# A two-layer graph attention kernel: sixteen early gathers are kept in SBUF until layer 1 begins, and their completion is placed anew over the groups

## The chip, the core and the metric

The kernel runs on one core of a Trainium2 chip. The time is the device time of one execution in microseconds. Before the change the median of five runs was 2100.81 us, the lowest 2096.71 and the highest 2101.95. Engines are named as in the profile: PE multiplies matrices, DVE and ACT work on vectors, POOL issues the gathers, and SP issues the plain transfers. Each engine takes its instructions in order, so whatever waits at the head of a queue holds up everything behind it.

## The reference

There are 6250 nodes with 768 features and 100000 edges, sorted by destination. The features are normalised and rectified, then pass through two attention convolutions, two dense layers and a residual:

```python
def gat_conv(x, src, dst, W, a_src, a_dst, bias, heads):
    h = (x @ W).reshape(n, heads, -1)
    e = leaky_relu(alpha_s[src] + alpha_d[dst], 0.2)     # per edge and head
    e = exp(e - segment_max(e, dst)[dst])
    alpha = e / (segment_sum(e, dst)[dst] + 1e-16)
    return segment_sum(h[src] * alpha[:, :, None], dst).reshape(n, -1) + bias

h = relu(layernorm(x))
h = relu(gat_conv(h, ..., heads=4))     # 768 -> 4 * 64, called layer 1
h = relu(gat_conv(h, ..., heads=1))     # 256 -> 256, called layer 2
out = x + relu(h @ Wm1 + bm1) @ Wm2 + bm2
```

Each layer also adds one loop edge per node. The costly access is `h[src]`, one row of a node table for every edge.

## The kernel before

**Tiles.** Nodes are cut into NT = 49 tiles of 128. Edges are cut into tiles of 128, two tiles make a pair, and four tiles make a group; there are 196 groups. Four groups belong to a node tile, with t the node tile and j the place of a group in it (g = 4t + j).

**The feature stage** is the loop over i in 0 to 48 at lines 509 to 552. It computes the rows `h` of node tile i on PE (line 447), scales them into `kept[i]` on ACT, and stores them from SP to the node table in DRAM (`store1`, line 474). SP also loads `x` eight tiles ahead (line 202) and its transposed copy `xT` five tiles ahead (line 410). In the program as built, SP's transfers share eight completion semaphores in turn, so an issue waits until the transfer eight places before it has landed. POOL's gathers have eight of their own.

**Layers 1 and 2** are both `layer_edges`. For every tile of 128 edges POOL issues one indirect DMA (`gather`, line 645), which fetches the 128 source rows into half of a pair buffer `G`. Gathers are issued `AHEAD` = 8 groups before their use. DVE forms the edge weights of a pair from its rows (lines 712 to 724), PE sums the rows by destination (line 736), and the finished node tiles go through `Node1.steps` or `Node2.steps`. The buffers `G` are one ring of 20 (`gathered`, line 257), which the early gathers of the next paragraph share.

**Early gathers (SOON).** POOL has little to do in the feature stage, so 23 pairs of layer 1 are gathered there. Pair i belongs to group 8i + 11. It is gathered as soon as only the first `SOON[i]` node tiles are in the table (`soon_rows`, line 352); an edge whose source is later fetches a row that is dropped afterwards. The number of tiles still missing runs from 20 down to 2, so the pairs are gathered one or two per iteration from i = 28 to i = 46. To free its buffer the pair is copied to DRAM (`soon_away`, line 360, from SP), and read back eight groups before its use (`soon_back`, line 364). In layer 1 each half of such a pair, numbered k = 2i and 2i + 1, is completed: SP fetches the source numbers (`soon_sources`, line 371), DVE compares them with the node numbers of the missing tiles (`soon_hits`, line 379), PE multiplies the resulting hits with the `kept` tiles (`soon_missing`, line 389), and DVE adds the product to the gathered rows (`soon_whole`, line 396).

**When the copies go out before.** In the feature stage a pair is copied out in the iteration that is `SOON_HELD` = 6 tiles after its gather, so from i = 34 on, right after the store of tile i. Of the 23 pairs, 18 are copied there. The other five are copied by `soon_away(NT)` at line 804, when layer 1 begins, behind the loads of layer 1's first tables.

**The order in SP's queue** in iteration i is: `x` of tile i + 8, `xT` of tile i + 5, the store of tile i, and then the copies. At the beginning of layer 1 it is: two weight loads (lines 924 and 170), three loads `drow` of the destination numbers (line 610), the source numbers of the first pair, the copies, the fourth `drow`, and four copies of edge masks (line 664).

**When the completion runs before.** Half k is completed over node tile t = k: hits at j = 0, the product at j = 2, and the addition at j = 1 of the next tile.

Of the kernel before, what the change touches and what calls it, by code (L numbers as in the profile page):

```python
# [27 lines left out]
NT = -(-N // P)  # L28
# [22 lines left out]

SOON = [NT - m for m in (11, 20, 2, 19, 11, 18, 3, 17, 4, 16, 4, 15, 5, 15, 6, 14, 7, 13, 8, 12, 9, 18,
                         10)]
SOON_AT = {2 * (8 * i + 11) + 1: i for i in range(len(SOON))}
SOON_FROM, SOON_HELD = min(SOON), 6
BARE = 8


# [11 lines left out]
def kernel(  # L70
# [21 lines left out]
    nc = tc.nc  # L92
# [11 lines left out]
    def bcast(src, n, off=0):  # L104

        return bass.AP(tensor=src.tensor, offset=src.offset + off, ap=[[0, P], [1, n]])
# [103 lines left out]
    def heads_row(row):  # L210
        return row[:, :RW[1]].rearrange("p (h c) -> p h c", h=4)
# [124 lines left out]
    soon_d = dram.tile([len(SOON), P, 2 * TW[1]], F32, name="soon_d")  # L336
    soon_G, soon_of, soon_p, soon_hit = {}, {}, {}, {}
    soon_pair = {i: pair for pair, i in SOON_AT.items()}

# [13 lines left out]
                        out=soon_G[i][:, t], out_offset=None, in_=table[1][:there * P],  # L353
                        in_offset=bass.IndirectOffsetOnAxis(ap=soon_i[:, i, t:t + 1], axis=0))

    def soon_away(there):

        for i in sorted(soon_G):
            if SOON[i] <= there:
                nc.sync.dma_start(soon_d[i], soon_G.pop(i).rearrange("p t c -> p (t c)"))  # L360

    def soon_back(i):
        G = rows_in(1)
# [3 lines left out]
    def soon_sources(pool, i):  # L367

        if i < len(SOON):
            soon_of[i] = pool.tile([P, 2 * P], I32, name="soon_of", bufs=2)  # L370
            nc.sync.dma_start(soon_of[i], bcast(src_rows, 2 * P, 2 * P * soon_pair[i]))

    def soon_hits(pool, k):

        i, t = divmod(k, 2)
        if i < len(SOON):
            m = NT - SOON[i]
            soon_hit[k] = pool.tile([P, NT - SOON_FROM, P], F32, name="soon_hit")
            nc.vector.tensor_tensor(  # L379
                soon_hit[k][:, :m],  # L380
                soon_of[i][:, t * P:(t + 1) * P].unsqueeze(1).to_broadcast([P, m, P]),
                nid_ps[:, SOON[i]:].unsqueeze(2).to_broadcast([P, m, P]), ALU.is_equal)

    def soon_missing(k):
        if 0 <= k < 2 * len(SOON):
            there, hit = SOON[k // 2], soon_hit.pop(k)
            soon_p[k] = ps.tile([P, TW[1]], F32, name="missing1", tag="n")
            for T in range(there, NT):
                nc.tensor.matmul(soon_p[k], hit[:, T - there], kept[T], start=(T == there),  # L389
                                 stop=(T == NT - 1))  # L390

    def soon_whole(G, k):
        if 0 <= k < 2 * len(SOON):
            i, t = divmod(k, 2)
            row = G[soon_pair[i]][:, t]
            nc.vector.scalar_tensor_tensor(row, row, soon_ok[:, i, t:t + 1], soon_p.pop(k),
                                           ALU.mult, ALU.add)
# [3 lines left out]
    with tc.tile_pool(name="w1p", bufs=1) as wp, tc.tile_pool(name="x1", bufs=6) as xp, \  # L401
# [3 lines left out]
        def fetch_x(i):  # L405
            xs[i], _ = load_x(xp, i)
# [102 lines left out]
        for i in range(NT):  # L509
            h = features1(i)  # L510
            if i == 0:
                centre(1)
                moments(2)
            elif i == 1:
                centre(2)
                moments(3)
                spread_means(3)
                moments(4)
            else:
                if i + 3 < NT:  # L520
                    moments(i + 3)
                if i + 2 < NT:
                    spread_means(i + 2)
                if i + 1 < NT:
                    centre(i + 1)
            if i == 0:
                fetch_x(6)
                fetch_x(7)
            if i + 8 < NT:
                fetch_x(i + 8)  # L530
            if i + 5 < NT:
                fetch_xT(i + 5)
            if i == 40:
                first_places()
            if 2 <= i < 2 + KI // 2:
                for k in range(2 * i - 4, 2 * i - 2):
                    nc.vector.tensor_reduce(w1[:, k, HID:], score_w[k], AX.X, ALU.add)
            if BARE <= i < 2 * BARE:
                scores1(i - BARE)
            keep1(i, *h)  # L540
            if 4 <= i < BARE + 4:
                halves[i - 4] = halve(heads_row(kept[i - 4])[:, :, :HID // 4])
            if BARE < i <= 2 * BARE:
                store1(i - BARE - 1)
            if BARE < i <= SOON_FROM - 3:
                store1(i - 1)
            if i >= SOON_FROM - 3:
                store1(i)
                soon_rows(i + 1)
                soon_away(i + 1 - SOON_HELD)  # L550
            if i >= 10:
                next(pieces, None)

# [65 lines left out]
    def layer_edges(layer, H, node, pre, matched, pre_pool):  # L619
# [4 lines left out]
        with tc.tile_pool(name=f"eg{layer}", bufs=5) as eg, \  # L624
# [3 lines left out]
            G, hot, e_ps, o_ps = {}, {}, {}, {}  # L628
# [5 lines left out]
            def gather(g):  # L634
                if not 0 <= g < NG:
                    return
                for t in tiles(g):
                    k = TPG * g + t
                    soon = layer == 1 and k // 2 in SOON_AT
                    if k // 2 not in G:  # L640
                        G[k // 2] = (soon_back(SOON_AT[k // 2]) if soon else
                                     first_G.get(layer, {}).get(k // 2) or rows_in(layer))
# [10 lines left out]
            def make_mask(u):  # L653

                if not 0 <= u < NU:
                    return
                if layer == 2:
                    return fetch_mask(u + 1)
                a, b = (t * P for t in both(u))
                mask[u] = maskp.tile([P, 8 * P], BF16, name="mask")  # L660
                at = u % 2 * 8 * P
                nc.vector.tensor_scalar(mask[u][:, a:b], drow[u // 2][:, at + a:at + b], pidx, None,
                                        ALU.is_equal)
                nc.sync.dma_start(mask_d[u * P:(u + 1) * P, a:b], mask[u][:, a:b])
# [135 lines left out]
            if layer == 1:  # L800
                for r in range(3):
                    fetch_rows(r)
                soon_sources(pre_pool, 0)
                soon_away(NT)
                fetch_rows(3)
                for u in range(4):
                    make_mask(u)
# [37 lines left out]
            for g in range(NG):  # L845
                t, j = divmod(g, 4)
                if layer == 2 and g >= NG - 2:
                    if g == NG - 2:
                        last_pairs()
                    continue  # L850
                if g == NG - 2:
                    at_end.append(g)
                gather(g + AHEAD)
                pair(g, 0)
                if g == NG - 1:
                    pair(g, 1)
                if g == NG - 2:
                    gather_up(NU - 2)
                advance(g)
                if taken_up(2 * g) is not None:  # L860
                    gather_up(taken_up(2 * g))
                if g <= NG - 4:
                    make_hot(g + 1)
                if g in (NG - 4, NG - 3):
                    make_hot(g + 2)
                if j == 0:
                    if layer == 1:
                        fetch_rows(t + 4)
                        if t % 2:
                            soon_sources(pre_pool, (t + 1) // 2)  # L870
                    node.prefetch(t)
                    meet(t + 1)
                    if layer == 1:
                        soon_hits(pre_pool, t)
                elif j == (2 if t < NT - 1 else 1):
                    node.ahead(t)
                    if layer == 1:
                        soon_missing(t)
                elif j % 2:
                    if layer == 1 and j == 1:  # L880
                        soon_whole(G, t - 1)
                    make_mask((g + 7) // 2)
                if g == NG - 3:
                    idle_ps.append(ps.tile([P, 4 * P], F32, name="idle_ps", tag="e"))
                if g >= NG - 3:
                    stay_warm(3)
                if g < NG - 1:
                    pair(g, 1)
                advance(g, 1)
                if j == 3:  # L890
                    join(t + 1)
                if taken_up(2 * g + 1) is not None:
                    gather_up(taken_up(2 * g + 1))
                if NG - 3 <= g < NG - 1:
                    stay_warm(3)
                hot.pop(g, None)
                if layer == 1 and g == NG - 6:
                    first_sources(2)
# [534 lines left out]
```

## Time and profile before

| what | value |
|---|---|
| median of five runs | 2100.81 us |
| the profiled execution | 2099.1 us |
| its span | 2097.3 us |
| PE busy | 1665.6 us (79%) |
| POOL busy | 1523.4 us (73%), 1666 instructions |
| DVE busy | 1412.2 us (67%) |
| ACT busy | 408.6 us (19%) |
| granted PE clock, mean | 0.889 |
| first gather of the feature stage | 99.31 us |
| first gather of layer 1 | 168.82 us |
| first gather of layer 2 | 1094.62 us |
| start of the last gather | 2073.61 us |

Times inside the execution count from the start of the span. The profile calls an engine busy only while an instruction runs on it; the time between two DMA issues of POOL that wait for nothing is shown as idle with the releaser "issue". A line of a timeline gives the start, the duration, the engine, the line of the code, the operation, what is written and read, the number of instructions merged, and in brackets the idle time ahead of it with what ended it. SPq is SP's queue.

### The profile page before, as it was taken

What the parts mean: (1) busy time and instruction counts of PE and PEld (TensorE: products, weight loads), DVE (VectorE), ACT (ScalarE), POOL (GpSimd) and SP (SyncE); (2) the same over time, 40 slices, a digit from 0 to 9 for tenths busy, and PEclk for the clock granted to TensorE, in tenths of its full rate; (3) what the DMA queues carried; (4) which work ended last, traced back from release to release, by engine and by line L of the source; (5) the groups of instructions that cost most, each with busy time, mean ns of one, the idle gap of its engine ahead of it and who ended that gap; (6) DMA issues with size and microseconds to landing.
All of it is one profiled execution on the core that took longest, in us unless ns stands there. A gap on an engine that the chain in (4) does not pass through costs nothing. (4 is left out here: it accounts for less than half of the span.)

```text
span 2097.3 us, 26497 instructions
## 1 busy us (share of the span) xinstructions
PE 1665.6 (79%) x7727; PEld 1212.1 (58%) x7729; DVE 1412.2 (67%) x4195; ACT 408.6 (19%) x1273; POOL 1523.4 (73%) x1666
## 2 busy tenths in 40 slices
PE   9986878887887888878867777778778777777877
PEld 6864756666665666666645545545455455454544
DVE  7856888888887888888876655555555555555554
ACT  5761111111111111111111111111111111111211
POOL 7057777777777777777777777777777777777774
PEclk9997999989998998999989888888888888888899
DMA  9998666666666666666557455555555555555553
GB/s 347 347 374 282 175 193 177 185 187 179 190 178 187 185 181 182 181 186 185 162 142 223 131 182 177 161 182 165 175 182 156 182 172 166 182 160 179 169 178 108
DMA packets 167328, 400.37 MB, mean 191 GB/s; under 512 B 36631, under 2 KB 54254, under 8 KB 167174
## 3 DMA queue, kind: packets, MB, share of 16 engines
q0 software_dynamic: 75072, 211.10, 37.6%
q1 hardware_dynamic: 90732, 185.99, 24.8%
q10 hardware_dynamic: 1370, 1.48, 0.2%
q8 instruction: 65, 1.06, 0.2%
q14 instruction: 89, 0.73, 0.1%
HBM read 333.87 MB, written 64.56 MB: 190 GB/s over the span
## 5 line engine op out<-in xcount | busy, mean ns | idle before, releaser
L645 POOL DMA_INDIRECT G<-table,src_i x1507 | 1431.3, 950 | 459.6 <-issue 325.6
L736 PE MATMUL o_ps<-G,hw 128*128 128x258 f32 x1564 | 463.6, 434 | 234.7 <-DVE hw L719 233.6
L736 PE MATMUL o_ps<-hw,hot 128*128 128x260 f32 x1564 | 454.3, 433 | 159.1 <-DVE hw L724 135.1
L736 PEld LDWEIGHTS o_ps<-G,hw 128*128 128x128 f32 x1564 | 315.5, 214 | 353.0 <-DVE hw L719 285.8
L712 DVE TENSOR_TENSOR e_ps<-G,e_ps 128x8 f32<-128x8 f32 (+1 forms) x782 | 129.1, 165 | 527.5 <-DMA G<-table,src_i 522.9
L736 PEld LDWEIGHTS o_ps<-hw,hot 128*128 128x128 f32 x1564 | 306.3, 208 | 275.1 <-DVE hw L724 193.1
L762 ACT ACTIVATE sum<-acc 32x260 f32<-32x260 f32 (+1 forms) x384 | 159.9, 416 | 1396.0 <-DVE acc L753 1335.2
L719 DVE TENSOR_SCALAR hw<-iota_ps,dcol,w 128x128 f32<-128x128 f32 x782 | 284.9, 406 | 14.5
L724 DVE TENSOR_TENSOR hw<-G,e_ps 128x520 f32<-128x520 f32 x391 | 271.9, 696 | 13.4
L389 PE MATMUL missing<-kept,soon_hit 128*128 128x268 f32 x1028 | 250.7, 402 | 0.0
L389 PEld LDWEIGHTS missing<-kept,soon_hit 128*128 128x128 f32 x1028 | 201.2, 200 | 37.0
L1085 PE MATMUL y_ps<-wm,mT 128*128 128x384 f32 x392 | 199.2, 643 | 0.0
L447 PE MATMUL h_ps<-w,r 128*128 128x264 f32 (+1 forms) x588 | 137.4, 387 | 10.0 <-ACT r L437 9.9
L673 DVE TENSOR_TENSOR hot<-iota_ps,dcol 128x512 f32<-128x512 f32 x196 | 133.5, 681 | 0.0
L447 PEld LDWEIGHTS h_ps<-w,r 128*128 128x128 f32 x588 | 108.3, 191 | 32.2 <-ACT r L437 13.2
L1085 PEld LDWEIGHTS y_ps<-wm,mT 128*128 128x128 f32 x392 | 85.8, 242 | 62.8 <-issue 38.6
L352 POOL DMA_INDIRECT G<-table,soon_i x46 | 43.9, 954 | 78.3 <-DMA xt<-in_x 53.0
L753 DVE SCALAR_TENSOR_TENSOR acc<-acc,keep,o_ps 128x260 f32<-128x260 f32 (+1 forms) x192 | 91.2, 475 | 0.9 <-PE o_ps L736 0.9
L379 DVE TENSOR_TENSOR soon_hit<-soon_of,iota_ps 128x1408 f32<-128x1408 int32 (+18 forms) x46 | 75.2, 1635 | 9.5 <-PE missing L389 9.5
L722 DVE TENSOR_TENSOR e_ps<-e_ps,G 128x8 f32<-128x8 f32 x391 | 68.0, 174 | 13.6 <-DVE e_ps L712 0.2
L715 DVE TENSOR_TENSOR w<-e_ps,G 128x2 f32<-128x2 f32 x391 | 62.1, 159 | 14.3 <-DVE e_ps L712 1.1
L435 DVE TENSOR_TENSOR cent<-xTt,mean_ps 128x768 f32<-128x768 f32 x49 | 46.6, 951 | 32.2 <-PE mean_ps L429 17.6
(415 smaller groups left out, 1180.4 us busy)
## 6 DMA issues: line engine op xcount, KB each, us to landing
xt<-in_x SPq DMA_DIRECT2D x96, 384.0 KB
drow<-dmod_d SPq DMA_DIRECT2D x49, 512.0 KB
mask_d<-mask SPq DMA_DIRECT2D x97, 256.0 KB
mask<-mask_d SPq DMA_DIRECT2D x97, 256.0 KB
G<-table,src_i POOLq DMA_INDIRECT x1507
xTt<-in_xT SPq DMA_DIRECT2D x49, 384.0 KB
out<-y SPq DMA_DIRECT2D x48, 384.0 KB
table<-kept SPq DMA_DIRECT2D x49, 134.0 KB
```

Source lines behind the costliest of these rows:

```text
L379: nc.vector.tensor_tensor(soon_hit[k][:, :m], soon_of[i][:, t * P:(t + 1) * P].unsqueeze(1).to_broadcast([P, m, P]), nid_ps[:, SOON[i]:].u ...
L389: nc.tensor.matmul(soon_p[k], hit[:, T - there], kept[T], start=(T == there), stop=(T == NT - 1))
L447: nc.tensor.matmul(h_ps[:, :n], r[:, k], w1[:, k, :n], start=(k == 0), stop=(k == KI - 1))
L645: nc.gpsimd.indirect_dma_start(out=G[k // 2][:, k % 2], out_offset=None, in_=table[layer], in_offset=bass.IndirectOffsetOnAxis(ap=src_i[:, ...
L673: nc.vector.tensor_tensor(hot[g][:, T[0]:T[0] + n], iota_ps.unsqueeze(1).to_broadcast([P, n, P]), dcol[:, k:k + n].unsqueeze(2).to_broadca ...
L712: nc.vector.tensor_mul(v, e2, rho)
L719: nc.vector.tensor_scalar(hw[:, t], iota_ps, dcol[:, k:k + 1], w[:, t], ALU.is_equal, ALU.mult)
L724: nc.vector.tensor_mul(hw, Gp[:, :, :RW[1]].rearrange("p t (h c) -> p t h c", h=H), w.unsqueeze(3).to_broadcast([P, 2, H, C + 1]))
L736: nc.tensor.matmul(o_ps[u], l, r[:, :RW[layer]], start=(g % 2 == 0 and k == 0), stop=(g % 2 == 1 and k == tiles(g)[-1]))
L753: nc.vector.scalar_tensor_tensor(acc, run[0], keep[:, u % 2:u % 2 + 1], o_ps.pop(u), ALU.mult, ALU.add)
L762: nc.scalar.activation(done[t][r], acc[r], AF.Copy)
L1085: nc.tensor.matmul(y_ps, mT[:, j], wm2[:, j, s * half:(s + 1) * half], start=False, stop=(j == KH - 1))
```

## The change

Three things change.

1. `soon_away` now takes the number of pairs that may stay. It copies out the oldest ones until no more than that are left. `SOON_HELD` becomes 16, so in the feature stage the first copy goes out in iteration 41, when the 17th pair is gathered; seven pairs are copied by iteration 46. The other 16 are copied when layer 1 begins, oldest first.
2. The steps that complete a half are tied to the group `at` = 8i + 11 of the pair rather than to the node tile. The source numbers are fetched at `at` - 13. The first half has its hits at `at` - 10, its product at `at` - 8 and its addition at `at` - 6; before these were at `at` - 11, - 9 and - 6. The second half has them at `at` - 6, - 5 and - 3; before at `at` - 7, - 5 and - 2. Hits therefore fall on groups with j = 1, where an edge mask is made too, and no longer on those with j = 0.
3. `dynamic_dma_scratch_size`, the bytes per SBUF partition reserved for the descriptors of POOL's DMAs, is 4096 and no longer 8192.

```diff
-SOON_AT = {2 * (8 * i + 11) + 1: i for i in range(len(SOON))}
-SOON_FROM, SOON_HELD = min(SOON), 6
+SOON_GROUP = [8 * i + 11 for i in range(len(SOON))]
+SOON_AT = {2 * g + 1: i for i, g in enumerate(SOON_GROUP)}
+SOON_FROM, SOON_HELD = min(SOON), 16
...
-    def soon_away(there):
-
-        for i in sorted(soon_G):
-            if SOON[i] <= there:
-                nc.sync.dma_start(soon_d[i], soon_G.pop(i).rearrange("p t c -> p (t c)"))
+    def soon_away(held):
+
+        for i in list(soon_G)[:max(len(soon_G) - held, 0)]:
+            nc.sync.dma_start(soon_d[i], soon_G.pop(i).rearrange("p t c -> p (t c)"))
...
-                soon_away(i + 1 - SOON_HELD)
+                soon_away(SOON_HELD)
...
-                soon_away(NT)
+                soon_away(0)
...
                     if layer == 1:
                         fetch_rows(t + 4)
-                        if t % 2:
-                            soon_sources(pre_pool, (t + 1) // 2)
                     node.prefetch(t)
                     meet(t + 1)
-                    if layer == 1:
-                        soon_hits(pre_pool, t)
                 elif j == (2 if t < NT - 1 else 1):
                     node.ahead(t)
-                    if layer == 1:
-                        soon_missing(t)
                 elif j % 2:
-                    if layer == 1 and j == 1:
-                        soon_whole(G, t - 1)
                     make_mask((g + 7) // 2)
+                if layer == 1:
+                    for i, at in enumerate(SOON_GROUP):
+                        for k, hits_at in ((2 * i, at - 10), (2 * i + 1, at - 6)):
+                            if g == hits_at + 3 + (k % 2 == 0):
+                                soon_whole(G, k)
+                            if g == hits_at:
+                                soon_hits(pre_pool, k)
+                            if g == hits_at + 1 + (k % 2 == 0):
+                                soon_missing(k)
+                        if g == at - 13:
+                            soon_sources(pre_pool, i)
...
-                   dynamic_dma_scratch_size=8192)
+                   dynamic_dma_scratch_size=4096)
```

## The prediction

> **What bounds the kernel now.** I read the costliest groups of the page first, then POOL's waits, then its timeline around the start of layer 1, and last SP's timeline, because the copies that move are SP's.
>
> ```profile
> L645 POOL DMA_INDIRECT G<-table,src_i x1507 | 1431.3, 950 | 459.6 <-issue 325.6
> L352 POOL DMA_INDIRECT G<-table,soon_i x46 | 43.9, 954 | 78.3 <-DMA xt<-in_x 53.0
> ```
> ```profile
> POOL G L645 <- issue: 325.6, 1067, 0.8
> ```
>
> A gather takes 0.95 us and POOL then idles 459.6 / 1507 = 0.305 us. Nearly every such gap is 0.3 us, in the timeline too, and the waits' list has none above 0.8 us for L645. So POOL issues one gather every 1.25 us from layer 1's start to the last at 2073.61 us and never waits for a buffer. DVE and PE follow the gathers: in three stretches of 100 us between 500 and 1000 us DVE waits 14.2 to 15.8 us for landing rows. The time is therefore when POOL's stream reaches layer 1, plus 1518 gathers (1507 of L645 and 11 of layer 2's first), plus a tail of some 23 us. What matters is the stretch ahead of that:
>
> ```profile
> 117.30 0.94 POOL L352 DMA_INDIRECT G<-table,soon_i  x1 [0.97 <-DVE mv L418]
> 129.31 0.94 POOL L352 DMA_INDIRECT G<-table,soon_i  x1 [2.25 <-DVE cent L435]
> 134.85 0.94 POOL L352 DMA_INDIRECT G<-table,soon_i  x1 [3.35 <-DMA table<-kept]
> 143.18 0.94 POOL L352 DMA_INDIRECT G<-table,soon_i  x1 [1.13 <-DVE cent L435]
> 148.26 0.94 POOL L352 DMA_INDIRECT G<-table,soon_i  x1 [2.88 <-DMA table<-kept]
> 151.12 0.94 POOL L352 DMA_INDIRECT G<-table,soon_i  x1 [0.67 <-DVE cent L435]
> 168.82 0.95 POOL L645 DMA_INDIRECT G<-table,src_i  x1 [0.30 <-issue]
> ```
>
> Here POOL does wait, for table rows that the feature stage brings late. The stage is short of DMA there (columns: us, PE, PEld, DVE, ACT and POOL busy, granted clock, DMA share, GB/s; then the wait itself):
>
> ```profile
> 110.00:120.00 10.00, 9.67 (x45) 7.66 (x44) 7.87 (x20) 7.80 (x24) 6.82 (x8) 1.00 1.04 395
> 130.00:140.00 10.00, 5.90 (x27) 4.48 (x26) 5.27 (x12) 4.03 (x15) 5.12 (x7) 1.00 1.05 355
> ```
> ```profile
> DVE cent L435 <- DMA xTt<-in_xT: 10.3, 5, 3.4
> ```
>
> PE falls from 9.67 us busy in 10 to 5.90 while the DMA engines stay full. SP's queue shows what came in between:
>
> ```profile
> 94.82 0.33 SPq L474 DMA_DIRECT2D table<-kept  x1
> 111.84 0.33 SPq L474 DMA_DIRECT2D table<-kept  x1
> 113.21 0.33 SPq L360 DMA_DIRECT2D soon_d<-G  x1
> 140.59 0.34 SPq L474 DMA_DIRECT2D table<-kept  x1
> 161.51 0.32 SPq L474 DMA_DIRECT2D table<-kept  x1
> 165.43 0.84 SPq L371 DMA_DIRECT2D soon_of<-in_src_rows  x1
> 173.86 3.00 SPq L360 DMA_DIRECT2D soon_d<-G  x5
> ```
>
> The stores of tiles 28 and 34 are 17.02 us apart, 2.84 us an iteration. Those of 34 and 40 are 28.75 us apart, 4.8 us each, and eight copies lie among them. Tile 48 is stored at 161.51 us.
>
> **Part 1a, copies taken out of the feature stage.** Of 18 copies 11 go; more to the point, up to the last load of `xT` (issued at 147.76 us) 11 copies were issued and 2 will be. The 9 are 268 KB each, 274 thousand bytes: 0.70 us at the 395 GB/s of the first window, 0.77 us at the 355 of the second, so 6.3 to 7.0 us of a full DMA, and 9 places in SP's queue. From above the gain is bounded by compute: 14 iterations from 111.84 us at 2.84 us put the last store at 151.6, 9.9 us earlier, and the wait on `xT` is 10.3 us in all. I take 8, nearer to the middle of 6.3 and 9.9: store of tile 48 at 153.5 us.
>
> What POOL makes of it: after 117.30 us there are 34 early gathers, which at 1.25 us end at 159.8; layer 1's first starts at 168.82. So 9.0 us is all there is to win (waits above their 0.3 us: 0.67 at 117.30 is kept, then 1.95 + 3.05 + 0.83 + 2.58 + 0.37 = 8.8, the rest a few longer gathers). Are the rows early enough for it? The tightest is tile 37. With iterations of 2.95 us its store is issued at 111.84 + 3 x 2.95 = 120.7; tile 40's store was released 7.7 us after its issue (140.59 to 148.26), so 128.4, and POOL comes to it at 117.30 + 10 x 1.25 = 129.8. The margin is 1.4 us; I leave 0.5 us for a wait. Layer 1's own first gather needs tile 48 stored: 153.5 plus some 5 is 158.5, just ahead of 159.8.
>
> **Part 1b, copies added where layer 1 begins.** SP issues 16 in place of 5. Five took 3.00 us, so 0.6 us each, +6.6 us; against it, SP stood from 166.3 to 173.86 because the first copy in order of i was the youngest pair, whose gathers had just been issued. Oldest first, it doesn't stand there. Behind the copies are the fourth `drow`, four mask copies and the first read-back, which SP reached at 176.96 us. With the later half of the copies paced by landings of about 1 us each, I expect it there at about 176 again. The `drow` landed some 7 us later and is needed for the seventh mask, made in group 5 (the sixth was at 192.69 us in group 3), so 185 against 195 even with layer 1 running 8 us earlier: free; without that cover each us would hold DVE by one, and POOL only after its two groups of spare buffers, 10 us.
>
> The copies also hold the buffers that layer 1 gathers into. The ring has 20. Layer 1's first four pairs take buffers freed by the seven early copies; the fifth waits for the first of the 16. POOL comes to it 8 gathers after 159.8, at 169.8. Now for when that copy lands:
>
> ```profile
> 171.50 1.01 DVE L662 TENSOR_SCALAR mask<-drow,pidx 128x1024 bf16<-128x1024 bf16 x2 [0.91 <-DMA drow<-dmod_d]
> 173.59 0.88 DVE L662 TENSOR_SCALAR mask<-drow,pidx 128x1024 bf16<-128x1024 bf16 x2 [1.07 <-DMA drow<-dmod_d]
> ```
>
> The first two `drow` land 2.1 us apart, so the third at 175.7, the source numbers behind it at about 176.3 and a copy 1 us later at 177.3, which is 15.8 us after the store of tile 48. From 153.5 that is 169.3: in time by 0.5 us. With the store at 155 it is a wait of 1 us, with no gain in part 1a one that cancels everything. The later pairs need one copy per 2.5 us and these land one per us. I charge 0.5 us (ends: 0 and 8).
>
> **Part 2, completion spread anew.** Nothing is added: 46 hits (1635 ns on average), 1028 products (402 ns) and 46 additions move by at most two groups. The first half's additions and the second's hits now share a group with a mask: 0.5 + 1.6 + 0.5 us on top of two pairs at 0.17 + 0.17 + 0.70 us, a `hot` of 0.68 and a sum of 0.48, so 5.8 us against 5.0 us of gathers, made up in the next groups, where DVE waits for rows. The 9.5 us that hits waited for products is off the path too. POOL, two groups of buffers ahead, doesn't see it: 0. Should DVE fall behind by more than 10 us, each further one counts.
>
> **Part 3, descriptor space halved.** No row shows what a gather takes of it. At the loaded start the semaphore updates show a gather landing 7.65 us after its issue, six in flight, and POOL not waiting; so 8192 bytes hold six at least, and 4096 three. At 1.25 us each, three cover 3.75 us, and gathers in layers 1 and 2 land 2.7 to 5.5 us after issue. The ends are therefore 0 and some 1 us on many gathers, hundreds of us. I take 0, as nothing marks the space before as nearly full.
>
> The Trainium skill (DMA: Bandwidth & Descriptors, "Terms" and "The descriptor swizzle") counts 8 data descriptors and one for completion per engine for a transfer over 128 partitions, at 16 bytes. By it, as an estimate, a gather takes 144 bytes of a ring and 4096 hold 28; the sum would be unchanged. No run here shows that count.
>
> **The sum.** -9.0 + 0.5 + 0.5 + 0 + 0 = -8.0 us. The profiled execution took 2099.1 us (span 2097.3 and 1.8 around it), so 2091.1; the median is 1.7 above it, 2092.8, said as 2093. The waits of 1.26 and 0.78 us where POOL enters layer 2 depend on layer 1's last rows, which shift with the gathers, and stay.
>
> **Rivals.**
> *Half of it.* The loads run no faster than halfway between, or the fifth pair waits 3 to 5 us. For it: the margins of 1.4 and 0.5 us. Against: the copies lie exactly where the pace drops. Gain 4.5: 2096.
> *No change.* DMA is busy to its share anyway and the other loads spread over the room. For it: the DMA share of 1.04 and more also at 110 us, where the pace was good. 2101.
> *The sixteen copies become the wait (slower).* Their place is the fifth to twelfth pair of layer 1. If SP's eight open transfers land together and not in turn, the first copy is some 7 us later. Without a gain in part 1a that is 184 against POOL's 178.8 before, 5.5 us lost: 2106. It decides from the point where the first copy lands after 178.8 us. Against it: the two `drow` land in turn.
> *Descriptor space* binds: 2200 and up.
>
> **How the numbers follow.** Forecast (gain 6.5 to 9.5) 0.57, half of it 0.20, no change 0.09, copies 0.10, descriptor space 0.04. By 0.2%, 4.2 us, about what this kernel's measurement can tell from no change, faster is 0.57 and over half of the second, 0.69; same 0.17; slower 0.14. The range runs from 2089.3 (all 9 us, and 2.5 for the spread of the runs) to 2099.5, which takes in the second case and the near half of the third.
>
> **What would show it.** Right: no wait over 0.5 us on POOL after 117 us in the feature stage, the store of tile 48 at 152 to 155 us, L645 starting at 160 to 161 and no gap at its ninth gather, then the same 1.25 us to the end. Wrong: PE still starved with `xT` late; a gap of several us at the ninth gather with a copy as its releaser; the gap between gathers above 0.3 us throughout (descriptor space); DVE late on whole rows so that POOL waits for a buffer in layer 1.

## The result, and the profile after

The changed kernel takes 2096.78 us (median of 31 runs, 2092.43 to 2099.53). The kernel before, beside it on the same chip, took 2100.8 (median of 53). The ratio is 0.9983 with a 95% interval of 0.9978 to 0.9988, so the gain is about 4 us, 2.5 to 4.6. The forecast was 2093, 8 us; the value that came is that of the rival "half of it". Four of the runs below, e5 to e8, were made on a chip where TensorE was granted 0.80 of its clock and every version took 2578 to 2599 us; they are read against each other alone.

First what didn't change. The first two lines are from the costliest groups of the changed kernel's page (busy us, mean ns of one | idle before, releaser), the third from its list of POOL's waits (total us, times, longest us).

```profile
L645 POOL DMA_INDIRECT G<-table,src_i x1507 | 1432.3, 950 | 460.6 <-issue 332.7
L353 POOL DMA_INDIRECT G<-table,soon_i x46 | 44.3, 963 | 74.3 <-DMA xTt<-in_xT 53.9
```
```profile
POOL G L645 <- issue: 332.7, 1087, 1.9
```

The gathers of layer 1 and most of layer 2 take 0.95 us with 0.306 us idle before each, as before. POOL still sets the time, and a gain can only be made ahead of layer 1 (or at the boundary to layer 2, or in the tail). Ahead of layer 1 the change did what was forecast, but not all of it. POOL's timeline of the changed kernel (start, duration, what; idle before and its releaser in brackets):

```profile
117.23 0.94 POOL L353 DMA_INDIRECT G<-table,soon_i  x1 [1.20 <-DVE mv L418]
...
131.97 0.94 POOL L353 DMA_INDIRECT G<-table,soon_i  x1 [2.54 <-DMA table<-kept]
...
137.92 0.94 POOL L353 DMA_INDIRECT G<-table,soon_i  x1 [1.26 <-DVE stats L416]
...
142.25 0.96 POOL L353 DMA_INDIRECT G<-table,soon_i  x1 [2.14 <-DVE stats L416]
...
152.57 0.94 POOL L353 DMA_INDIRECT G<-table,soon_i  x1 [0.62 <-DVE cent L435]
...
165.16 0.95 POOL L645 DMA_INDIRECT G<-table,src_i  x1 [0.30 <-issue]
...
175.17 0.95 POOL L645 DMA_INDIRECT G<-table,src_i  x1 [0.30 <-issue]
```

Layer 1's first gather starts at 165.16 us instead of 168.82. Four waits are left behind 117.23, 2.24 + 0.96 + 1.84 + 0.32 = 5.4 us above the usual 0.30; before there were 8.8. And the ninth gather of layer 1, at 175.17, has no gap. SP's timeline of the changed kernel shows the stores of table rows and the copies (L360):

```profile
111.86 0.33 SPq L474 DMA_DIRECT2D table<-kept  x1
...
122.51 0.33 SPq L474 DMA_DIRECT2D table<-kept  x1
...
135.84 0.34 SPq L474 DMA_DIRECT2D table<-kept  x1
138.19 0.33 SPq L474 DMA_DIRECT2D table<-kept  x1
140.27 0.33 SPq L360 DMA_DIRECT2D soon_d<-G  x1
...
154.98 2.99 SPq L474 DMA_DIRECT2D table<-kept  x2
...
161.57 16.86 SPq L360 DMA_DIRECT2D soon_d<-G  x16
179.13 0.32 SPq L610 DMA_DIRECT2D drow<-dmod_d  x1
```

The first copy is now issued at 140.27 us. Yet the stores of tiles 34 and 40 (111.86 and 135.84) are 24.0 us apart, 4.0 us an iteration in place of 4.8, and not 2.84; the copies cannot be what holds them. Tile 48, the second store of the pair at 154.98, is stored at 157.6 us, 3.9 earlier than before. The two lines on which the prediction rested read like this in the changed kernel (110 to 165 us for the wait):

```profile
130.00:140.00 10.00, 6.52 (x25) 4.91 (x24) 4.18 (x8) 4.11 (x14) 5.55 (x6) 0.86 1.02 291
```
```profile
DVE cent L435 <- DMA xTt<-in_xT: 7.9, 4, 3.6
```

PE is busy 6.52 us of these ten where it was 5.90, and the wait on `xT` has gone from 10.3 to 7.9 us. The DMA engines are full as before, at 291 GB/s in place of 355.

Behind layer 1 the two recorded executions differ once more, by things of the same size. At the boundary to layer 2 POOL waits 1.85 and 1.87 us, against 1.26 and 0.78 (the kernel before first):

```profile
1098.10 0.94 POOL L330 DMA_INDIRECT G<-table,first_i  x1 [1.26 <-DVE kept L968]
...
1110.32 0.94 POOL L645 DMA_INDIRECT G<-table,src_i  x1 [0.78 <-issue]
```
```profile
1096.20 0.94 POOL L331 DMA_INDIRECT G<-table,first_i  x1 [1.85 <-DVE kept L971]
...
1109.29 0.94 POOL L645 DMA_INDIRECT G<-table,src_i  x1 [1.87 <-issue]
```

These two waits cost 1.7 us more, and the 1507 gathers of L645 were busy 1.0 us longer in all. The last gather is thus only 1.1 us earlier (2072.5 against 2073.6); the profiled span is still 3.8 us shorter (2093.5 against 2097.3), because the tail behind that gather is 2.7 us shorter. In the tail of the recorded execution before, eight transposes (L1075) took 2.08 us together against 1.16 after; the granted clock was 0.74 from 2075 to 2085 us there, and 1.00 from 2071 to 2081 us after. The change doesn't touch them.

### The profile page after: what moved, and what is told of

It reads as the page before. It is cut to its first block, busy times and chain, and to the rows that moved or that the text cites. A ratio compares the mean times of both kernels' runs of the same rounds, so it can differ in the third digit from the quotient of the medians.

```text
span 2093.5 us, 26527 instructions
## 1 busy us (share of the span) xinstructions
PE 1675.8 (80%) x7727; PEld 1219.7 (58%) x7729; DVE 1409.3 (67%) x4195; ACT 408.4 (20%) x1273; POOL 1524.6 (73%) x1666
## 5 line engine op out<-in xcount | busy, mean ns | idle before, releaser
L645 POOL DMA_INDIRECT G<-table,src_i x1507 | 1432.3, 950 | 460.6 <-issue 332.7
L736 PE MATMUL o_ps<-hw,hot 128*128 128x260 f32 x1564 | 467.9, 442 | 153.5 <-DVE hw L724 138.9
L736 PEld LDWEIGHTS o_ps<-hw,hot 128*128 128x128 f32 x1564 | 314.8, 214 | 270.2 <-DVE hw L724 190.4
L1088 PEld LDWEIGHTS y_ps<-wm,mT 128*128 128x128 f32 x392 | 86.1, 243 | 62.8 <-issue 38.3
L921 ACT ACTIVATE rT<-tp,bT 128x128 f32<-128x128 f32 x196 | 61.2, 363 | 27.3 <-PE tp L915 26.2
```

The lines of the kernel that those rows point to most:

```text
L645: nc.gpsimd.indirect_dma_start(out=G[k // 2][:, k % 2], out_offset=None, in_=table[layer], in_offset=bass.IndirectOffsetOnAxis(ap=src_i[:, ...
L736: nc.tensor.matmul(o_ps[u], l, r[:, :RW[layer]], start=(g % 2 == 0 and k == 0), stop=(g % 2 == 1 and k == tiles(g)[-1]))
L1088: nc.tensor.matmul(y_ps, mT[:, j], wm2[:, j, s * half:(s + 1) * half], start=False, stop=(j == KH - 1))
```

## The experiments

Two questions stood: which part of the change gave the gain, and why the feature stage stays at 4 us an iteration from 126 to 142 us with the copies gone.

**e1: holding the copies alone.** The kernel before with this edit; completion and descriptor space stay as they were.

```diff
-SOON_FROM, SOON_HELD = min(SOON), 6
+SOON_FROM, SOON_HELD = min(SOON), 16
...
-    def soon_away(there):
-        for i in sorted(soon_G):
-            if SOON[i] <= there:
-                nc.sync.dma_start(soon_d[i], ...)
+    def soon_away(held):
+        for i in list(soon_G)[:max(len(soon_G) - held, 0)]:
+            nc.sync.dma_start(soon_d[i], ...)
...
-                soon_away(i + 1 - SOON_HELD)
+                soon_away(SOON_HELD)
...
-                soon_away(NT)
+                soon_away(0)
```

> Only the copies are held back; the completion and the descriptor space are as before. Theory (the gain is DMA time freed in the feature stage): ratio to before 0.998, about 4 us less, layer 1's first gather at about 165 us as in the changed kernel. Rival (the new placement of the completion, or the smaller descriptor space, gives or takes part of it): a ratio that differs from 0.9983 by more than the intervals, 0.9965 if the other parts cost 4 us, 1.000 if they gave the gain.

Measured: 2098.81 us against 2102.88, ratio 0.9983 [0.9974, 0.9992], the same as for the whole change. Layer 1's first gather is at 165.9 us, store of tile 48 at 158.2.

**e2: the other two parts alone.** The changed kernel with the copies as before.

```diff
-SOON_FROM, SOON_HELD = min(SOON), 16
+SOON_FROM, SOON_HELD = min(SOON), 6
```

(and `soon_away` as before)

> The complement: the new completion and 4096 bytes of descriptor space, with the copies where they were before. Theory: 1.000, layer 1's first gather at 168 to 169 us, gaps of 0.3 us between gathers. Rival (these parts matter): away from 1.000 by 0.002, and then POOL waits in layer 1 that before does not have.

Measured: 2103.06 against 2102.88, 1.0009 [1.0000, 1.0018]. The new completion and the halved descriptor space give nothing and cost at most 4 us; together with e1, the gain is that of the copies (held back, and at layer 1's start sent oldest first; these two were not tried apart).

**e4: eleven pairs held** in place of 16 (`SOON_HELD = 11`).

> The changed kernel with 11 pairs held in place of 16, so that copies begin in iteration 37 and not 41, and 7 rather than 2 of them are issued ahead of the last load of the transposed features (11 before). Theory (each copy ahead of those loads costs the same): 4 of 9 copies less, so 4/9 of 4 us, ratio 0.9991, layer 1's first gather at about 167 us. Rival (only the number that wait at layer 1's start, or the order of the copies there, matters): 0.998 as with 16, or 1.000.

Measured: 2101.9, 0.9996 [0.9987, 1.0005]; first gather of layer 1 at 168.2 us. By the medians, holding five fewer pairs gives back most of the gain; the interval holds the 0.9991 of the theory and no gain at all, so e4 doesn't show that each copy costs the same. With e1 it supports that the gain comes from the copies that no longer go ahead of the loads. A copy takes bytes and a place in SP's queue, and no run keeps the one and removes the other; what the table under e9 says of the rates speaks for the bytes.

**e3: the store of small pieces out of the stage.** In the profiles DMA slows down for some microseconds at about 130 us, 4 to 5 us behind the store of the output bias in 384 pieces of 12 bytes. Here that store is moved to the middle of layer 1 (the moved tiles are left out).

```diff
-        nc.sync.dma_start(bm2_d.rearrange("s (p k) -> p s k", p=P), bp)
...
+                if layer == 1 and g == NG // 2:
+                    nc.sync.dma_start(bm2_d.rearrange("s (p k) -> p s k", p=P), bp)
```

> The changed kernel, with the store of the last bias (384 pieces of 12 bytes) moved from the feature stage, where it lands at 131 us, to the middle of layer 1. Theory A (this store in small pieces is what slows all DMA between 130 and 140 us, where the rate falls to 265 and 318 GB/s, and so kept half of the predicted gain back): the rate stays above 355 GB/s there, tile 48 is stored at 153 to 155 us, layer 1's first gather comes at 161 to 162 us, and the time is 3 to 4 us below the changed kernel, ratio to before 0.9965. Rival B (the slow stretch is the gathers' and loads' own): the stretch stays, 0.998.

Measured: 2097.64, 0.9975 [0.9964, 0.9987]. The stretch did not go: the store of tile 48 is at 157.5 us and layer 1's first gather at 164.5, as in the changed kernel (157.6 and 165.2). The ratio cannot be told from the changed kernel's.

**e5 to e8: the kernels before and after again, and two further edits**, on the chip with the clock of 0.80. e7 moves the bias's load (128 pieces of 24 bytes) too, with the five DVE operations that split it into parts:

```diff
-        nc.sync.dma_start(b, bm2.rearrange("(p k) -> p k", p=P))
...
-        in_parts(nc.vector, [bp[:, k] for k in range(3)], b, rest[:, 0], rest[:, 1])
...
+                if layer == 1 and g == NG // 2 - 8:
+                    nc.sync.dma_start(b, bm2.rearrange("(p k) -> p k", p=P))
+                if layer == 1 and g == NG // 2:
+                    in_parts(nc.vector, [bp[:, k] for k in range(3)], b, brest[:, 0], brest[:, 1])
...
```

e8 is e7 with the last tile of `x` read in one transfer, as the last 128 rows; the 106 nodes of tile 48 then get the means of other rows:

```diff
-        if n < P:
-            nc.vector.memset(t, 0.0)
-        for a, b in runs(n):
-            nc.sync.dma_start(t[a:b], x[i * P + a:i * P + b])
+        n0 = min(i * P, N - P)
+        nc.sync.dma_start(t, x[n0:n0 + P])
```

> The kernel before, profiled a second time, to see how far one execution's feature stage stands for the others. In the recorded executions the store of tile 48 went from 161.5 us (before) to 157.6 us (after), 3.9 us, although 2.57 MB less were moved between 110 us and that store (18.64 against 16.07 MB), 6.5 us at 395 GB/s. The packets that took longer than the median of their size cost 3.9 us of all 16 DMA engines in that stretch before and 5.7 us after. Theory 1 (the lost time belongs to the stage and grows when the copies are gone, so that it eats 2 us of the gain): the store of tile 48 at 161 to 162 us again, about 4 us lost. Theory 2 (the lost time scatters from execution to execution by 2 to 3 us and the recorded execution of the kernel before was a lucky one): the store at 163 to 165 us, 5 to 7 us lost.

> The changed kernel a second time, profiled and timed beside the runs below. Ratio to the kernel before 0.998 under both theories. Theory 1: store of tile 48 at 157 to 158.5 us with 5 to 6 us lost to slow packets. Theory 2: anywhere from 155 to 159 us, with 3 to 6 us lost.

> The changed kernel with the two transfers of small pieces taken out of the feature stage: the load of the output bias (128 pieces of 24 bytes, issued at 100.8 us) and the store of its parts (384 pieces of 12 bytes, issued at 123.1 us) are done in the middle of layer 1. Theory C (these small pieces make the DMA engines slow for the 3 to 5 us in which they are worked off: every profile so far has a slow stretch some 2 us behind the load, at 102 to 107 us, and 4 to 5 us behind the store): both stretches go, 370 GB/s or more from 100 to 108 and from 125 to 135 us; the store of tile 48 2 us earlier than in the changed kernel, at 155 to 156 us; ratio to the kernel before 0.9972 to 0.9976. Rival D (the slow stretches come from gathers, loads and stores of rows meeting in memory): both stretches stay, the ratio is that of the changed kernel, 0.998.

> As the run with the small pieces moved, and besides the last tile of x is read as the last 128 rows in one transfer instead of 96 and 10 rows in two (the 106 rows of tile 48 then get the means of other rows: that part of the computation is changed). A second slow stretch has stood 4 to 8 us behind the 10-row transfer in every profile (142 to 145 us before, 136 to 140 after). If the split makes it: no slow stretch between 135 and 148 us, under 1 us lost there in place of 1.5 to 2, the store of tile 48 at 154 to 155 us, ratio 0.0005 below that run. If not: the stretch stays and the ratio is the same.

Measured: e5 2598.9 us in one run; against a kernel before of 2592.0 us e6 is 0.9972 [0.9954, 0.9989], e7 0.9951 [0.9929, 0.9973], e8 0.9946 [0.9925, 0.9967]. The changed kernel is faster there too. For the question they say little: on that chip the feature stage stands still for 5 to 8 us at a time, and POOL alone does not set the pace. The group of gathers in e6 has nearly twice the idle time of the changed kernel's 460.6 us:

```profile
L645 POOL DMA_INDIRECT G<-table,src_i x1507 | 1438.0, 954 | 870.3 <-issue 390.6
```

One thing could be used: the stretch at 102 to 107 us was still there in e7 and e8, 275 to 315 GB/s from 102.5 to 107.5, although the 24-byte load was no longer in it. So that load is not its cause. The intervals of e6, e7 and e8 overlap; whether the split of the last tile costs anything is open.

**e9: the kernel before, profiled once more.**

> The kernel before, profiled once more, because the group of e5 to e8 ran where the granted clock was 0.80 and the whole kernel took 2592 us, with stalls of 5 to 8 us in the feature stage, so that e5 says nothing of the executions at 2101 us. Theory 1 (the lost DMA time grows when the copies are gone): store of tile 48 at 161 to 162 us, about 4 us lost to slow packets between 110 us and that store. Theory 2 (it scatters, and the first recorded execution was a lucky one; with the copies as before and all else changed it was 165.8 us with 7.2 us lost): store at 163 to 166 us, 5 to 7 us lost.

Measured: 2102.79 us, store of tile 48 at 164.8, layer 1's first gather at 171.0. This is what theory 2 expected: the lost time scatters, and the execution shown as "before" was a lucky one in the feature stage (it took 2099.1 us, 1.7 below its median). It rests on this one execution, with e2, whose copies are as before, beside it. The next table puts the executions side by side. "Lost" is worked out from the trace's DMA packets: for each packet the time above the usual one of its size (9 ns for 4 and 12 bytes, 48 for 1072, 84 for 2048, 87 for 2144, 121 for 3072, 168 for 4288), summed and divided by 16 engines, from 110 us to 2 us ahead of the store of tile 48; MB is what was moved in that time.

| execution | first early gather | store of tile 48 | layer 1's first gather | MB | lost us |
|---|---|---|---|---|---|
| before | 99.3 | 161.5 | 168.8 | 18.65 | 3.9 |
| e9, before again | 99.6 | 164.8 | 171.0 | 18.78 | 6.4 |
| e2, copies as before | 100.3 | 165.8 | 173.6 | 18.75 | 7.2 |
| e4, eleven held | 99.8 | 160.5 | 168.2 | 17.49 | 5.5 |
| after | 100.2 | 157.6 | 165.2 | 16.08 | 5.7 |
| e1, copies held | 100.4 | 158.2 | 165.9 | 16.09 | 6.4 |
| e3, bias store later | 99.8 | 157.5 | 164.5 | 16.28 | 5.3 |
| e10, small pieces later | 100.2 | 157.8 | 164.4 | 16.27 | 5.4 |
| e11, row 0 spread | 106.0 | 160.6 | 167.9 | 17.85 | 4.8 |
| e12, small pieces later and row 0 spread | 100.0 | 154.9 | 162.7 | 15.92 | 3.9 |

The first three, with copies, reach layer 1 at 168.8 to 173.6 us; after, e1, e3 and e10, with the copies held, at 164.4 to 165.9. The last gather of all starts at 2073.6 to 2081.0 us in the first group and at 2070.6 to 2073.2 in the second. The bytes agree with the copies taken out: 2.6 MB are 6.6 us at 395 GB/s. Divided by the time in which they were moved they give 349 to 356 GB/s in e9 and e2 and 348 to 358 in after, e1, e3 and e10: with copies and without, the stage took as long as its bytes at one rate. Only the first execution before stands out, with 377. The time lost to slow packets shows no dependence on the copies. It scatters by 3 us from one execution to the next.

**e10: both small transfers later**, the kernel of e7 where the clock is 0.88.

> The kernel of e7 again, for the same reason. Theory C (the pieces of 24 and 12 bytes make the slow stretches): 370 GB/s or more from 125 to 135 us, store of tile 48 at 155 to 156 us, ratio to the kernel before 0.9972 to 0.9976. The stretch at 102 to 107 us stayed in e7 and e8 though the 24-byte load was gone from it, so that half of C has fallen and this stretch is expected to stay. Rival D (rows meeting in memory): both stretches stay, 0.998.

Measured: 2095.76 against 2102.18, 0.9970 [0.9958, 0.9982]. Theory C (the two small transfers make the slow stretches) is not borne out: the store of tile 48 stays at 157.8 us. The ratio lies below the changed kernel's 0.9983 [0.9978, 0.9988], but the intervals overlap. The difference of the two is 1.3 thousandths with an uncertainty as large, so the small pieces cost between nothing and some 5 us.

**e11: the missing sources read different rows.** An early gather whose source isn't stored yet reads row 0, and is multiplied by 0 later. Here it reads the row of its partition number.

```diff
         nc.vector.tensor_tensor(soon_i[:, i], of, soon_ok[:, i], ALU.mult)
+        own = const.tile([P, 2], I32, name=f"soon_own{i}")
+        nc.vector.tensor_scalar(own, of, float(SOON[i] * P), pidx[:, 0:1], ALU.is_ge, ALU.mult)
+        nc.vector.tensor_tensor(soon_i[:, i], soon_i[:, i], own, ALU.add)
```

> The changed kernel, but an early gather whose source isn't stored yet reads the table row of its own partition number (0 to 127) in place of row 0; it is multiplied by 0 either way. Of the 128 rows of the first early gathers about 41% (20 of 49 tiles missing) are now all row 0. Theory H (many reads of one row hold the DMA engines up): the slow stretch that begins some 2 us after the first early gather, 102 to 107 us, goes (380 GB/s), and some of the later ones; store of tile 48 at 154 to 156 us, ratio to the kernel before 0.997. If one row is no hindrance: the stretch stays and the ratio is 0.998.

Measured: 2101.82, 0.9998 [0.9989, 1.0006], no gain, for a reason that none of the theories had. The two groups that the edit added, from DVE's list of groups between 20 and 90 us, and the first early gather of e11 in POOL's timeline:

```profile
L347 DVE TENSOR_SCALAR soon_own<-src_i,pidx 128x2 int32<-128x2 int32 x23 | 5.1, 223 | 0.0
...
L348 DVE CUSTOM_DVE_ANT_0 soon_i<-soon_i,soon_own 128x4 uint16<-128x4 uint16 x23 | 3.7, 161 | 0.8
```
```profile
105.99 1.13 POOL L356 DMA_INDIRECT G<-table,soon_i  x1 [59.61 <-DMA xTt<-in_xT]
```

DVE got 8.8 us of work ahead of the first early gather, and that gather came 5.8 us late. But from there to layer 1's first gather e11 took 61.9 us, against 65.0 in the changed kernel, and the 8 us behind the first early gather lost 0.8 us to slow packets, where the eight other executions of before, after, e1 to e4, e9 and e10 lost 1.4 to 1.8.

**e12: the same end without further DVE work**, on top of e10. The number of stored rows is taken off an index that isn't stored yet, and POOL makes the factor of 0 or 1.

```diff
-        nc.vector.tensor_scalar(soon_ok[:, i], of, float(SOON[i] * P), None, ALU.is_lt)
-        nc.vector.tensor_tensor(soon_i[:, i], of, soon_ok[:, i], ALU.mult)
+        nc.gpsimd.tensor_scalar(soon_ok[:, i], of, float(SOON[i] * P), None, ALU.is_lt)
+        back = const.tile([P, 2], I32, name=f"soon_back{i}")
+        nc.vector.tensor_scalar(back, of, float(SOON[i] * P), -float(SOON[i] * P), ALU.is_ge, ALU.mult)
+        nc.vector.tensor_tensor(soon_i[:, i], of, back, ALU.add)
```

> e10 with the reads of row 0 taken out in another way, since e11's 46 further DVE operations in the first 90 us made the stage some 5 us late before any early gather was issued (first early gather at 106.0 instead of 100.2 us). Here an index that isn't stored yet has the number of stored rows taken off, so that the missing sources read different stored rows; DVE keeps its two operations per pair, and the comparison that makes the factor moves to POOL. From its first early gather to layer 1's first gather e11 took 61.9 us, against 65.0 in the changed kernel and 64.2 in e10. Theory H (many reads of one row hold the DMA engines up): again 62 us, layer 1's first gather at 162 to 163 us, and a ratio to the kernel before of 0.996, below both kernels and e10. If e11's shorter stretch came from its late start alone (the loads had run further ahead of the gathers): 64 to 65 us and 0.997, like e10.

Measured: 2094.05 us against 2102.75, ratio 0.9955 [0.9942, 0.9969], some 9 us faster than before. This interval lies below the changed kernel's: e12 beats both kernels. Behind 117 us its POOL timeline keeps waits of at most 0.8 us above the 0.30, 2.8 us in all, where the changed kernel had up to 2.2 and 5.4 in all. It has one of 2.48 us ahead of that, which the changed kernel doesn't have:

```profile
107.41 0.95 POOL L349 DMA_INDIRECT G<-table,soon_i  x1 [2.48 <-DVE cent L431]
...
130.52 0.94 POOL L349 DMA_INDIRECT G<-table,soon_i  x1 [0.85 <-DVE cent L431]
...
138.64 0.95 POOL L349 DMA_INDIRECT G<-table,soon_i  x1 [0.93 <-DVE stats L412]
...
147.72 0.94 POOL L349 DMA_INDIRECT G<-table,soon_i  x1 [1.11 <-DVE cent L431]
...
162.72 1.12 POOL L641 DMA_INDIRECT G<-table,src_i  x1 [0.30 <-issue]
```

The windows set the stretches beside one another (columns: us, PE, PEld, DVE, ACT and POOL busy, granted clock, DMA share, GB/s). First the changed kernel, then e9, then e10, then e12, and at last the kernel before and e11:

```profile
100.00:108.00 8.00, 7.94 (x38) 6.43 (x37) 6.27 (x13) 6.32 (x21) 6.11 (x6) 1.00 1.01 312
110.00:125.00 15.00, 14.67 (x68) 11.89 (x67) 11.92 (x28) 11.93 (x38) 10.31 (x12) 1.00 1.03 380
125.00:150.00 25.00, 21.35 (x90) 16.88 (x89) 13.52 (x28) 13.84 (x47) 15.10 (x17) 0.93 1.03 336
```
```profile
100.00:108.00 8.00, 7.94 (x38) 6.44 (x37) 6.28 (x13) 6.33 (x21) 4.79 (x5) 1.00 1.02 315
...
125.00:150.00 25.00, 17.49 (x69) 12.82 (x67) 12.52 (x27) 10.41 (x36) 11.33 (x12) 0.93 1.03 332
```
```profile
100.00:108.00 8.00, 7.93 (x37) 6.43 (x36) 6.51 (x13) 6.49 (x22) 5.35 (x6) 1.00 1.02 321
...
125.00:150.00 25.00, 21.67 (x91) 17.23 (x90) 14.25 (x29) 14.24 (x48) 16.93 (x19) 0.93 1.03 349
```
```profile
100.00:108.00 8.00, 7.93 (x38) 6.46 (x37) 6.60 (x13) 6.65 (x22) 4.61 (x5) 1.00 1.00 344
110.00:125.00 15.00, 14.67 (x68) 11.88 (x67) 11.30 (x23) 11.97 (x40) 11.35 (x13) 1.00 1.04 390
125.00:150.00 25.00, 22.97 (x105) 18.48 (x104) 14.81 (x30) 15.68 (x53) 17.00 (x18) 1.00 1.05 369
```
```profile
125.00:150.00 25.00, 16.34 (x72) 12.59 (x71) 12.24 (x28) 11.37 (x41) 12.64 (x14) 1.00 1.05 363
```
```profile
125.00:150.00 25.00, 22.34 (x101) 17.87 (x100) 16.64 (x34) 16.18 (x56) 16.30 (x18) 1.00 1.04 348
```

The DMA share is 1.00 to 1.05 in every line. What differs is GB/s: 332 to 349 from 125 to 150 us in the first three, 369 in e12, so full DMA engines moved 5 to 10% less in the three than in e12. This window alone says nothing of row 0, though: the first execution before reads it and has 363, and e11 doesn't and has 348.

How far is theory H shown, that many reads of one row hold the DMA engines up? Two edits that take the many reads of row 0 away, made in different ways, both shorten the way from the first early gather to layer 1 (61.9 and 62.8 us; 64.2 to 65.4 in after, e1, e3 and e10) and both bring the loss in the 8 us behind the first early gather down to 0.8 and 0.9 us. That speaks for it, from one execution of each; over the whole stretch of the table the loss in e12, 3.9 us, is that of the first execution before, and in e6, on the other chip, those 8 us lost 1.1. Against e10 alone, e12's time is 0.9955 to 0.9970, and these two intervals overlap. The share of row 0 in e12's gain, and that of the small pieces, are therefore not separated; shown is that both together are faster than the change. A stretch from 132.5 to 137.5 us stayed in e12 as well, 298 and 325 GB/s in its two halves, and its cause is open.

## Why the prediction was right, and where it was not

The time fell, for the reason given and by half of the amount: 2096.8 us lies in the stated range, at the value of the rival that had 0.20. Of the four marks set for being right only the last came, no gap at layer 1's ninth gather and the same 1.25 us to the end. The store of tile 48 (157.6 for 152 to 155), layer 1's first gather (165.2 for 160 to 161) and POOL's waits (up to 2.54 for 0.5) missed theirs. The first mark of being wrong, PE short of `xT`, came in part: 7.9 us of waiting are left of 10.3.

**What bounds the kernel.** Right. POOL's pace of 1.25 us a gather is the same to the end. That the recorded pair differs by 3.8 us, just what was won ahead of layer 1, is luck: 2.5 us were lost again on the way to the last gather, and 2.7 came from the tail, and neither was forecast. The last gathers of all the executions, above, are the better evidence.

**Part 1a, the term of -9.0 us for POOL and the 8 us for the store of tile 48.** The mechanism was right (e1, e2, e4), the size was not: the store moved by 3.9 us and layer 1's first gather by 3.7 in the recorded executions, and the times by 4.0. Three things went wrong in this term.

- "8, nearer to the middle of 6.3 and 9.9" stood between a bound by bytes and one by compute, as if the stage had become half bound by compute. It remained bound by DMA, with a share of 1.03 from 125 to 150 us and PE busy 21.35 of 25: 2.6 MB less is 6.6 us. The lower end was the better estimate.
- The rate that turned bytes into time was taken as steady, 355 to 395 GB/s, and the whole loss of pace was put down to the copies. The line I showed for 130 to 140 us already held the counter-evidence: a DMA share of 1.05 with 355 GB/s, against 1.04 with 395 at 110. In these ten microseconds slow packets took 1.3 us of all engines, from 110 to 120 us 0.3. The engines were full in both windows, so the lower rate is not a matter of how much there was to move. Slow packets cost 5.7 and 6.4 us in the executions with the copies held and the small transfers left alone (after, e1).
- One execution was the base. Its stage had lost 3.9 us, while e9 and e2 lost 6.4 and 7.2. Measured from those, the store moved by 7 to 8 us, as forecast; measured from the one recorded, by 3.9. But e2's profiled execution took 2106.3 us, 3.2 above its median, so it is no fair base either. The medians over many runs say 4.0 [2.5, 4.6], below the 6.6 us of the bytes; where the rest went is open, since the scatter between executions is as large.

**The row that decides.** The step on tile 37 named the right place. Its gather was forecast at 129.8 us with the rows at 128.4. The rows' store was issued at 122.51, not 120.7 (the iterations took 3.55 us, not 2.95), and landed at 131.2. That gather is the one at 131.97 with the wait of 2.54 us, 9.5 us behind the store's issue, where the 7.7 taken from 140.59 to 148.26 was the same measure. A margin of 1.4 us stood against an error in pace and landing of 3.6. The 0.5 us set aside for it should have been some 2, and three more waits followed, 0.96, 1.84 and 0.32 us above the usual, which the profile puts down to DVE.

**Part 1b, 0.5 us for the fifth pair.** It cost nothing: no gap at 175.17. The first of the sixteen copies had landed at about 171.2 us, 13.6 us behind the store of tile 48 where I had 15.8, and POOL came later than forecast. SP issued the sixteen in 16.86 us, paced by landings of about 1.05 us, and reached the fourth `drow` at 179.13 in place of about 176; nobody waited for it. The rival in which the copies become the wait is out.

**Parts 2 and 3, 0 each.** Right within e2's interval, which reaches from 0 to 3.8 us. The idle time between gathers is 0.306 us with half the descriptor space, so the rival of the descriptor space is out. As an aside, the Trainium skill's count (DMA: Bandwidth & Descriptors, "The descriptor swizzle") leaves room for 28 gathers by the estimate in the prediction; no run here shows the count, only that no gather waited.

**The waits at the boundary** were to stay at 1.26 and 0.78 and became 1.85 and 1.87. From layer 1's last gather to layer 2's first own one the three executions with the old completion take 16.8 to 17.2 us (before, e9, e1), the seven with the new one 17.2 to 19.0, 18.0 on average. So the new completion or the smaller descriptor space seems to cost about 1 us here; no run tells which, and the ratio of e1 equals that of the whole change.

## What to carry to other kernels

A DMA share near 1 says that the engines are occupied and not that they move bytes: read it beside GB/s, and where the rate falls at a full share, removing transfers may give back less than their bytes at the best rate seen (here 4.0 us of 6.6 by the medians). When the base is one profiled execution, profile it once more before a stage of it is priced; here the same kernel reached layer 1 at 168.8 and 171.0 us. Where placeholders are gathered, it is worth trying not to let them all be one row (not shown by itself here), and to make their indices without work for an engine that early gathers wait for.

## What the runs showed of the hardware

A packet of 3072 bytes takes 121 ns as a rule and now and then 0.5 to 2.6 us, in bursts of 2 to 6 us. In single microseconds the time above the usual reached 0.8 to 1.0 of all the engines' time (e1 and e4 from 130 to 131 us, e2 from 136 to 137; a packet counts where it starts). The Trainium skill (DMA: Bandwidth & Descriptors, "Latency and other measured facts") gives 2 us for an access to HBM under high load; the longest packets of ten executions between 100 and 160 us, 1.7 to 2.7 us, are of that size, though no run shows that they are such accesses. Its "Specifications" put the least transfer for the full rate at 512 bytes; moving the transfers of 12 and 24 bytes away left the bursts in place here (e3, e10).

The chip of e5 to e8 granted TensorE 0.80 of its clock where the others granted 0.88, and the kernel before took 2592 us in place of 2102. The gather itself took the same 0.95 us there; the idle time between gathers went from 460 to 870 us (changed kernel and e6), so a kernel that is paced by POOL on one chip was in part paced by other engines on the next.
